# Moving the second image's group statistics into the first image's last tiles, and splitting the last tiles' value products

## The chip, the cores and the metric

The kernel runs on one core of a Trainium2 chip. Its time is the device time of one execution in microseconds (us). The median of three runs is given, and one further execution is recorded by the hardware profiler. A difference of about 0.2% can be told from none.

## The reference, cut to what matters

Two images of 256 channels and 64 x 64 positions, fp32, pass through two residual layers, each on the group-normalised x:

```python
def _gn(v, G=32, eps=1e-5):              # 32 groups of 8 channels
    g = v.reshape(B_, G, C_ // G, H_, W_)
    m = jnp.mean(g, axis=(2, 3, 4), keepdims=True)
    s = jnp.var(g, axis=(2, 3, 4), keepdims=True)
    return ((g - m) / jnp.sqrt(s + eps)).reshape(v.shape)

# layer 0: 8 heads of 32 channels over all 4096 positions
qkv = jnp.einsum('bchw,oc->bohw', x, qkv_w) + qkv_b[None, :, None, None]
...
attn_weights = jax.nn.softmax(attn_logits, axis=-1)
out = jnp.einsum('bhij,bhcj->bhci', attn_weights, v)

# layer 1: two attentions in small blocks, and a convolution
ctx = _sa(blockify(fq), blockify(fk), blockify(v), oh, ow)   # 64 positions of equal place in the 8 x 8 blocks
feats = _bn_relu(_c1x1(ctx, lr_W_w), lr_W_scale, lr_W_shift)
...
qx = _bn_relu(_c1x1(_bn_relu(_c1x1(feats, sr_fq1_w), ...), sr_fq2_w), ...)
kx = _bn_relu(_c1x1(_bn_relu(_c1x1(feats, sr_fk1_w), ...), sr_fk2_w), ...)
vx = _c1x1(feats, sr_fv_w)
ctx2 = _sa(qx, kx, vx, DH, DW)                               # within each 8 x 8 block
feats2 = _bn_relu(_c1x1(ctx2, sr_W_w), sr_W_scale, sr_W_shift)
...
return rate1 * out_att + rate2 * out_conv                    # out_conv: 3 x 3 convolution of q, k, v

x = x + _L0_conv_ref(_gn(x), L0_conv_qkv_w, L0_conv_qkv_b, 8)
x = x + _L1_conv_ref(_gn(x), ...)
```

## The kernel before

The images are done one after the other. An image is held as eight tiles `x_b_t` of 128 partitions x 2 channel halves x 512 positions (eight rows of the picture), from `xpool`, which has nine buffers; so tiles of the second image can be loaded as those of the first come free.

Per image the stages are these. `group_stats` takes bn_stats (L321) of each half tile, 16 in all, aggregates them (L325), sums over the eight channels of a group with a small product on TensorE (`pm`, L328), forms the spread on VectorE (L328, L332 to L334), sums that over the group (`pv`, L337), and takes Sqrt on ScalarE (ACT, L340) and a reciprocal (L341). `normalise` (L366) then writes `xn`, 16 instructions. `project0` makes `p_wk` and `p_wq` (L416), `attention0` is the long attention over 4096 positions (L545, L551, L560, L597). `layer1_first` makes the first block attention, and `layer1_second` the rest: the second block attention in eight tiles t, and the convolution in 16 turns of `conv_step` (a strip s of a quarter of the image, and one of four output phases q), with the normalised image in `xp`. `xn` and `xp` share the single buffer of `apool`.

A tile of `layer1_second` goes so, by its names on TensorE: `phq`, `prq` (two products for the queries, L1354 and L1363, each followed by a ReLU on ACT, L1142), a turn of the convolution, `phk`, `prk` (the keys), `sp` (scores, L1081), `pvs` (values, L1060), a second turn, `at` (two transposes of the softmax, L1111), `pc` (softmax times values, L1129, one product for each half m of the channels, each followed by a ReLU into `res` on ACT), a third turn. The softmax lies between: maximum and subtraction on VectorE (L1099, L1101), exp on ACT (L1102), sum, reciprocal and product on VectorE (L1104 to L1106). `bd` copies (L1120) bring the transposes to SBUF. Values are copied from their bank half by half, on ACT (L1065) or VectorE (L1067). Tile 7 of the first image has one turn only, the last (strip 3, q 3), and tile 7 of the second has none.

A turn is eight matmuls times four (`mm`, L996), for which POOL makes the operand (`col`, L982, and `v`, L986) one turn ahead; afterwards ACT copies a part (L1001), VectorE makes `z` (L1002 to L1005) and adds it to two x tiles (L1017, L1021, L1023). ACT adds the border's corrections (`conv_edges`, L1030). When a strip's four turns are done, `give` (L1330) adds the attention's `res` to x, and SP writes it out.

The order is written out by hand for TensorE alone (`tc.manual_schedule`, inside `layer1_second`); on the other engines a scheduler orders the instructions, with `tc.issue_after` as a bound from below. The work for the second image that belongs to the seam is the generator `following`: its steps are taken in tile 7 of the first image, the first (loads, the 16 statistics and the aggregates) before `at`, the second (`pm`, the spread) between the two `pc` products, through the argument `between` of `group_attention`, and the third (`pv`, Sqrt, reciprocal) behind them. PSUM in `layer1_second` is four banks for `mm` and four for all else; `project0` has eight.

Of the kernel before, what the change touches and what calls it, by code (L numbers as in the profile page):

```python
# [40 lines left out]
def direct_layers(ctx: ExitStack, tc: tile.TileContext, a: dict, out: bass.AP, bad: bass.AP):  # L41
# [17 lines left out]
    def w4(shape, name, dtype=F32):  # L59
        return work.tile(shape, dtype, tag="w4", name=name)  # L60
# [4 lines left out]

    def load_x(b):
        tiles = []
        for t in range(NT):
            xt = xpool.tile([P, KC, T], F32, tag="x", name=f"x_{b}_{t}")
            nc.sync.dma_start(  # L70
                out=xt,
                in_=a["x"][b, :, t * T : (t + 1) * T].rearrange("(k p) n -> p k n", p=P),
            )
            tiles.append(xt)
        return tiles
# [912 lines left out]

    def conv_step(b, xts, wf, v, s, q, pacc):


        mm = pacc.tile([P, 2, 4, STRIP], F32, tag="acc", name=f"mm_{b}_{s}_{q}")
        for r in range(4):
            for m in range(2):
                for k in range(KC):
                    nc.tensor.matmul(  # L996
                        mm[:, m, r, :], wf[:, k, 4 * r + q, m * P : (m + 1) * P], v[r // 2][:, r % 2, k, :],
                        start=k == 0, stop=k == KC - 1,
                    )
        z = w4([P, 2, 2, STRIP], f"z_{b}_{s}_{q}")  # L1000
        nc.scalar.copy(z[:, 1], mm[:, :, 1, :])  # L1001
# [44 lines left out]

    def group_attention(nm, q, k, tokens, wv, out, busy=False, apart=False, more=None, between=None):

# [6 lines left out]

        def values(half):
            pv = bank([P, 2, C], f"pvs_{nm}_{half}")
            for i in range(2):
                for c in range(KC):
                    nc.tensor.matmul(  # L1060
                        pv[:, i, :], tokens(c, 2 * half + i), wv[:, c, :], start=c == 0, stop=c == KC - 1
                    )
            dst = vs[:, 2 * half : 2 * half + 2, :]
            if half == 0 or busy or apart:
                nc.scalar.copy(dst, pv)  # L1065
            else:
                nc.vector.tensor_copy(dst, pv)  # L1067
# [4 lines left out]

        sp = bank([P, 4, 64], f"sp_{nm}")
        def place_of(t, par):
            return sp[64 * par : 64 * par + 64, t, :], slice((4 * par + t) * 64, (4 * par + t) * 64 + 64)
# [18 lines left out]
        if not first:  # L1094
            values(0)
        if not apart:
            values(1)
# [25 lines left out]
        if apart:  # L1123
            values(1)
        yield
        for m in range(KC):
            pc = bank([P, T], f"pc_{nm}_{m}")
            for w in range(4):
                nc.tensor.matmul(  # L1129
                    pc[:, w * P : (w + 1) * P], vs[:, w, m * P : (m + 1) * P],  # L1130
                    bd[:, w].rearrange("p a i -> p (a i)"), start=True, stop=True,
                )
            out(m, pc)
            if m == 0 and between:
                between()

# [147 lines left out]
    def layer1_second(b, xts, feats, mean, rstd, shift, pacc, following):  # L1284
# [30 lines left out]

        def conv():
            nonlocal done, wf
            if wf is None:
                wf = fetch_conv_weights(b)
            if done + 1 < len(turns):  # L1320
                ahead[done + 1] = conv_transform(b, xp, *turns[done + 1])
            conv_step(b, xts, wf, ahead.pop(done), *turns[done], pacc)
            done += 1

        def give(n):
# [3 lines left out]
            for m in range(KC):  # L1329
                kept["given"] = nc.vector.scalar_tensor_tensor(  # L1330
                    res[:, m, :], res[:, m, :], wts["rate1"], xts[n][:, m, :], ALU.mult, ALU.add
                )
                if final:
                    (nc.scalar if m else nc.sync).dma_start(out=halves[:, m, :], in_=res[:, m, :])
# [9 lines left out]
        for t in range(NT):  # L1344
# [4 lines left out]

            def branch(one, two, col1, col2, nm):  # L1350
                hid = w4([P, KC, T], f"h{nm}_{nt}")
                ph = [bank([P, T], f"ph{nm}_{nt}_{m}") for m in range(KC)]
                for k, m in ((0, 0), (0, 1), (1, 0), (1, 1)) if t == 0 else ((0, 0), (1, 0), (0, 1), (1, 1)):
# [3 lines left out]
                    if k == KC - 1:  # L1357
                        bn_relu(hid[:, m, :], ph[m], col1, m)
                res = w4([P, KC, T], f"r{nm}_{nt}")
                pr = [bank([P, T], f"pr{nm}_{nt}_{m}") for m in range(KC)]  # L1360
# [8 lines left out]

            with tc.manual_schedule(engines={mybir.EngineType.PE}):  # L1370
                q = branch("fq1", "fq2", V_FQ1, V_FQ2, "q")
# [6 lines left out]
                if 0 in spots.get(t, ()) and (b or t > 2):  # L1378
                    conv()
                if b == 0 and t == NT - 1:  # L1380
                    for n in sorted(results):
                        give(n)
                k = branch("fk1", "fk2", V_FK1, V_FK2, "k")
                if b == 0 and t == 2:
# [3 lines left out]
                def to_res(m, pc, res=res):  # L1388
# [7 lines left out]
                    nt, q, k, lambda c, w, f=f: f[c][:, w * P : (w + 1) * P], wts["fv"], to_res, apart=t + 1 < NT,  # L1396
                    between=lambda: next(then) if b == 0 and t == NT - 1 else None,
                )
                next(parts)
                if 1 in spots.get(t, ()):  # L1400
                    conv()
                if t < 2 and b == 0:
                    pending = parts
                else:
                    next(parts)
                    if b == 0 and t == NT - 1:
                        next(then)
                    next(parts, None)
                    if b == 0 and t == NT - 1:
                        next(then)  # L1410
                if 2 in spots.get(t, ()):
                    conv()
            if b == 0 and t == 1:
# [13 lines left out]
            for n in sorted(n for n in results if done >= 4 * (n // 2 + 1)):  # L1427
                give(n)


    ahead = {}

    def following():

        ahead.update(xts=load_x(1), w0=load_layer0(1))
        with tc.issue_after(kept["given"].ins):
            steps = group_stats(ahead["xts"], "l0_1")
            next(steps)
        yield
        next(steps)  # L1440
        yield
        ahead["stats"] = next(steps)
        yield

    for b in range(B):
        xts = x_first if b == 0 else ahead["xts"]
        w0 = w0_first if b == 0 else ahead["w0"]
        with tc.tile_pool(name=f"ps0_{b}", bufs=8, space=PSUM) as psum["ps"]:
            mean, rstd = list(group_stats(xts, "l0_0"))[-1] if b == 0 else ahead["stats"]
            xn = apool.tile([P, KC, N], F32, tag="A", name=f"xn_{b}")  # L1450
            for t in range(NT):
                for k in range(KC):
                    normalised = normalise(xn[:, k, t * T : (t + 1) * T], xts[t][:, k, :], k, mean, rstd)
            fold = fold_scores() if b == 0 else iter(())
            next(fold, None)
            held = project0(b, xn, w0)
            next(fold, None)
# [570 lines left out]
```

## Time and profile before

| what | us |
|---|---|
| median of three runs (lowest to highest) | 3057.96 (3056.49 to 3058.67) |
| the profiled execution, its own time | 3062.01 |
| span of its trace, first to last instruction | 3060.1 |
| TensorE busy in the span | 2979.3 |
| VectorE, ScalarE, POOL busy | 2455.9, 2340.2, 832.1 |
| last turn of the first image on TensorE, start | 1520.23 |
| first product of the second image, start | 1552.39 |
| last `pc` of the second image, start | 3049.04 |

The mean granted clock of TensorE is 0.991. In the lines of the profile PE is TensorE, DVE VectorE, ACT ScalarE, SP the engine whose queue carries most transfers, and L with a number is the line in the kernel's text. In a timeline the columns are the start, the time taken, the engine and line, the operation with what it writes and reads, how many instructions are put together in the row, and in brackets how long the engine stood idle before them and what it waited for. TensorE is busy for 97% of the span, so a microsecond counts if TensorE stands still in it, or works slower than at full clock.

### The profile page before, as it was taken

The numbers are of one execution on the slowest core, as the hardware profiler recorded it, in microseconds if no ns is written. First come the engines' busy times: TensorE is split into PE (matmuls) and PEld (weight loads), VectorE is DVE, ScalarE is ACT, GpSimd is POOL, SyncE is SP. The second block draws the span as 40 slices with busy tenths as digits, with TensorE's granted clock in tenths as the row PEclk, the third lists the DMA queues.
The fourth block names the chain that finished last, engine by engine and source line by source line (L and its number), as shares of the span: only waits on it lengthen the run. The fifth ranks groups of instructions, "written<-read, shape, count | busy, mean of one in ns | idle before, by whom it ended". The sixth has DMA issues, their size and how long they took to land. (4 is left out here: it accounts for less than half of the span.)

```text
span 3060.1 us, 63941 instructions
## 1 busy us (share of the span) xinstructions
PE 2979.3 (97%) x25129; PEld 1859.9 (61%) x25129; DVE 2455.9 (80%) x3122; ACT 2340.2 (76%) x3266; POOL 832.1 (27%) x918
## 2 busy tenths in 40 slices
PE   7999999999999999999989999999999999999998
PEld 4565556655556556577755555666555565576765
DVE  4598998989899999856556989989988899835543
ACT  2699999999999984623237999999999999834333
POOL 1022222322223230155301222222222222306440
PEclk9999999999999999999999999999999999999999
DMA  7978789787897661230159787797878976700000
GB/s 259 274 137 180 150 163 175 153 172 157 176 181 159 140 135 42 73 131 28 42 193 274 134 169 163 159 181 146 174 162 167 183 160 131 170 5 4 21 15 22
DMA packets 244149, 425.01 MB, mean 139 GB/s; under 512 B 98889, under 2 KB 109949, under 8 KB 241661
## 3 DMA queue, kind: packets, MB, share of 16 engines
q0 software_dynamic: 94720, 237.57, 40.2%
q1 hardware_dynamic: 148972, 182.99, 21.6%
q8 instruction: 199, 3.26, 0.4%
q14 instruction: 114, 0.93, 0.1%
q10 hardware_dynamic: 144, 0.26, 0.0%
HBM read 119.55 MB, written 68.39 MB: 61 GB/s over the span
## 5 line engine op out<-in xcount | busy, mean ns | idle before, releaser
L551 ACT ACTIVATE es<-ring 128x512 f32<-128x512 f32 (+2 forms) x1572 | 1203.1, 904 | 29.9 <-PE ring L545 21.7
L545 PE MATMUL ring<-q,k 128*128 128x512 f32 x4096 | 1081.8, 407 | 11.2 <-ACT v L551 4.9
L597 DVE TENSOR_TENSOR e<-e,es 128x1024 f32<-128x1024 f32 (+1 forms) x956 | 1036.2, 1148 | 22.5 <-ACT es L551 22.2
L545 PEld LDWEIGHTS ring<-q,k 128*128 128x128 f32 x4096 | 733.4, 188 | 379.7 <-ACT es L551 115.7
L551 ACT ACTIVATE v<-ring 128x512 f32<-128x512 f32 (+2 forms) x1024 | 780.4, 899 | 23.8 <-PE ring L545 13.4
L560 PE MATMUL av<-es,v 128*32 128x256 f32 (+1 forms) x9684 | 725.2, 389 | 0.0
L597 DVE TENSOR_TENSOR e<-e,v 128x1024 f32<-128x1024 f32 (+1 forms) x636 | 670.1, 1112 | 22.4 <-ACT v L551 21.5
L560 PE MATMUL av<-v 128*32 128x256 f32 (+1 forms) x6188 | 498.0, 389 | 0.0
L560 PEld LDWEIGHTS av<-es,v 128*32 128x32 f32 x9684 | 328.3, 109 | 265.3 <-issue 105.5
L560 PEld LDWEIGHTS av<-v 128*32 128x32 f32 x6188 | 221.2, 109 | 171.2 <-issue 72.8
L996 PE MATMUL mm<-v,wf 128*128 128x256 f32 x1024 | 227.6, 380 | 1.5 <-DVE z L1005 1.5
L607 POOL DMA_DIRECT2D es<-es x118 | 100.7, 853 | 461.6 <-ACT es L551 411.4
L996 PEld LDWEIGHTS mm<-v,wf 128*128 128x128 f32 x1024 | 193.3, 190 | 36.8 <-issue 9.8
L986 POOL TENSOR_TENSOR v<-col 128x512 f32<-128x512 f32 x128 | 165.7, 1319 | 178.4 <-ACT rk_sr L1142 38.7
L1001 ACT COPY z<-mm 128x512 f32<-128x512 f32 x32 | 18.7, 586 | 183.3 <-PE mm L996 183.3
L607 POOL DMA_DIRECT2D acc<-es x118 | 119.5, 1018 | 113.8 <-ACT v L551 35.2
L605 POOL DMA_DIRECT2D es<-es x20 | 11.4, 569 | 495.2 <-ACT es L551 404.6
L607 POOL DMA_DIRECT2D es<-v x72 | 61.3, 852 | 290.8 <-ACT v L551 287.2
L1002 DVE TENSOR_TENSOR z<-z,mm 128x512 f32<-128x512 f32 x32 | 22.0, 687 | 140.1 <-ACT z L1001 139.7
L607 POOL DMA_DIRECT2D v<-es x112 | 114.3, 1020 | 17.7 <-ACT es L551 8.4
L607 POOL DMA_DIRECT2D acc<-v x78 | 75.1, 963 | 76.0 <-ACT es L551 31.1
L982 POOL TENSOR_TENSOR col<-xp 128x1152 f32<-128x1152 f32 x32 | 69.6, 2174 | 66.5 <-DVE xp L1420 55.1
(254 smaller groups left out, 2665.5 us busy)
## 6 DMA issues: line engine op xcount, KB each, us to landing
acc<-es POOLq DMA_DIRECT2D x128, 512.0 KB, 6.4
acc<-v POOLq DMA_DIRECT2D x84, 512.0 KB, 6.2
es<-es POOLq DMA_DIRECT2D x138, 256.0 KB, 4.3
v<-es POOLq DMA_DIRECT2D x132, 256.0 KB, 5.1
k<-wk_halves SPq DMA_DIRECT2D x64, 512.0 KB
q<-wq_halves SPq DMA_DIRECT2D x256, 128.0 KB
v<-v POOLq DMA_DIRECT2D x90, 256.0 KB, 5.0
es<-v POOLq DMA_DIRECT2D x84, 256.0 KB, 3.9
```

The source lines that it names most:

```text
L545: touch(nc.tensor.matmul(sc[:, i, :], held["k", g // 2][:, j * P : (j + 1) * P], held["q", g, u // 2][:, u % 2, :], start=True, stop=True, ...
L551: nc.scalar.activation(dst, sc, AF.Exp, scale=SC0), set(range(at % BANKS, at % BANKS + m))
L560: note(nc.tensor.matmul(dst[HD0 * u : HD0 * u + HD0, n], lhs, rhs(u)[:, n], start=start, stop=stop))
L597: nc.vector.tensor_add(dst[:, s, :], dst[:, s, :], src)
L605: nc.gpsimd.dma_start(out=dst, in_=src)
L607: nc.gpsimd.dma_start(out=dst, in_=src, accum_op=ALU.add)
L982: (nc.gpsimd.tensor_add if plus else nc.gpsimd.tensor_sub)(col, cols(one), cols(two))
L986: (nc.gpsimd.tensor_add if plus else nc.gpsimd.tensor_sub)(dst, rows(one), rows(two))
L996: nc.tensor.matmul(mm[:, m, r, :], wf[:, k, 4 * r + q, m * P : (m + 1) * P], v[r // 2][:, r % 2, k, :], start=k == 0, stop=k == KC - 1,)
L1001: nc.scalar.copy(z[:, 1], mm[:, :, 1, :])
L1002: nc.vector.tensor_add(z[:, 0], z[:, 1], mm[:, :, 0, :])
```

## The change

`following` becomes a generator of many small steps, which the tiles 6 and 7 of the first image take at fixed places. In these two tiles the order on VectorE is written out as well as that on TensorE. The tiles 0 to 6 of the second image are loaded ahead as before, and its tile 7 is read straight into the last part of `xn`, where it is normalised in place; a second copy of it goes into an x tile later, for the residual sum. The statistics come in three lots: tiles 0 to 2 in tile 6 after the scores, tiles 3 to 6 ahead of the `z` of turn 14, and tile 7 with the aggregates and the mean ahead of the `z` of turn 15. `pv`, Sqrt and reciprocal follow the key's first product, and the 16 normalises stand at several places in tile 7's attention: five before the maximum, one after the softmax's product, and so on.

In tile 7 of both images the value products are split around the transposes: three of the four places before, the last one behind the copies of `bd`, and ACT copies both halves. In most other tiles, the second `bd` copy stands ahead of the `z` of the turn that follows it.

In the program that comes of it, tile 7's two statistics stand with the first lot on VectorE and both aggregates with the second; the third lot is the mean and the spread. ACT has two table loads in tile 7 of the first image, and none at the start of the second image's attention. The five fetches of layer 0's weights stand earlier on POOL's queue, and the fetches of `k` on SP's stand ahead of six of the writes of `q`'s halves.

```diff
...
@@ -63,9 +63,9 @@
         return psum["ps"].tile(shape, F32, tag="bank", name=name)
 
 
-    def load_x(b):
+    def load_x(b, ts=range(NT)):
         tiles = []
-        for t in range(NT):
+        for t in ts:
             xt = xpool.tile([P, KC, T], F32, tag="x", name=f"x_{b}_{t}")
             nc.sync.dma_start(
                 out=xt,
@@ -986,7 +986,7 @@
             (nc.gpsimd.tensor_add if plus else nc.gpsimd.tensor_sub)(dst, rows(one), rows(two))
         return v
 
-    def conv_step(b, xts, wf, v, s, q, pacc):
+    def conv_step(b, xts, wf, v, s, q, pacc, behind_products=None):
 
 
         mm = pacc.tile([P, 2, 4, STRIP], F32, tag="acc", name=f"mm_{b}_{s}_{q}")
@@ -997,6 +997,8 @@
                         mm[:, m, r, :], wf[:, k, 4 * r + q, m * P : (m + 1) * P], v[r // 2][:, r % 2, k, :],
                         start=k == 0, stop=k == KC - 1,
                     )
+        if behind_products:
+            behind_products()
         z = w4([P, 2, 2, STRIP], f"z_{b}_{s}_{q}")
         nc.scalar.copy(z[:, 1], mm[:, :, 1, :])
         nc.vector.tensor_add(z[:, 0], z[:, 1], mm[:, :, 0, :])
@@ -1044,7 +1046,7 @@
 
     SC1 = C ** -0.5
 
-    def group_attention(nm, q, k, tokens, wv, out, busy=False, apart=False, more=None, between=None):
+    def group_attention(nm, q, k, tokens, wv, out, busy=False, apart=False, more=None, split=False, fill=None):
 
 
 
@@ -1053,15 +1055,21 @@
 
         vs = w4([P, 4, C], f"vs_{nm}")
 
-        def values(half):
-            pv = bank([P, 2, C], f"pvs_{nm}_{half}")
-            for i in range(2):
+        pvs = {}
+
+        def values(half, places=range(2)):
+            if half not in pvs:
+                pvs[half] = bank([P, 2, C], f"pvs_{nm}_{half}")
+            pv = pvs[half]
+            for i in places:
                 for c in range(KC):
                     nc.tensor.matmul(
                         pv[:, i, :], tokens(c, 2 * half + i), wv[:, c, :], start=c == 0, stop=c == KC - 1
                     )
+            if places[-1] == 0:
+                return
             dst = vs[:, 2 * half : 2 * half + 2, :]
-            if half == 0 or busy or apart:
+            if half == 0 or busy or apart or split:
                 nc.scalar.copy(dst, pv)
             else:
                 nc.vector.tensor_copy(dst, pv)
@@ -1071,6 +1079,7 @@
             values(0)
 
         sp = bank([P, 4, 64], f"sp_{nm}")
+
         def place_of(t, par):
             return sp[64 * par : 64 * par + 64, t, :], slice((4 * par + t) * 64, (4 * par + t) * 64 + 64)
 
@@ -1093,7 +1102,9 @@
             yield
         if not first:
             values(0)
-        if not apart:
+        if split:
+            values(1, range(1))
+        elif not apart:
             values(1)
         nm4 = small.tile([P, 4], F32, tag="nm4", name=f"nm4_{nm}")
         nc.vector.tensor_reduce(nm4, sp, AX.X, ALU.max, negate=True)
@@ -1122,6 +1133,8 @@
             )
         if apart:
             values(1)
+        elif split:
+            values(1, range(1, 2))
         yield
         for m in range(KC):
             pc = bank([P, T], f"pc_{nm}_{m}")
@@ -1131,8 +1144,8 @@
                     bd[:, w].rearrange("p a i -> p (a i)"), start=True, stop=True,
                 )
             out(m, pc)
-            if m == 0 and between:
-                between()
+            if fill:
+                fill(m)
 
     def product(pt, wt, src, m, last=True):
         for k in range(KC):
@@ -1313,13 +1326,13 @@
         }
         images = {1: range(5), 3: (5, 6), 4: (7,)} if b == 0 else {0: (3, 4), 1: (5,), 2: (6,), 3: (7,)}
 
-        def conv():
+        def conv(behind_products=None):
             nonlocal done, wf
             if wf is None:
                 wf = fetch_conv_weights(b)
             if done + 1 < len(turns):
                 ahead[done + 1] = conv_transform(b, xp, *turns[done + 1])
-            conv_step(b, xts, wf, ahead.pop(done), *turns[done], pacc)
+            conv_step(b, xts, wf, ahead.pop(done), *turns[done], pacc, behind_products)
             done += 1
 
         def give(n):
...
@@ -1347,7 +1360,7 @@
                 feats[k][:, 8 * t : 8 * t + 8].rearrange("p o d e -> p (o d e)") for k in range(KC)
             ]
 
-            def branch(one, two, col1, col2, nm):
+            def branch(one, two, col1, col2, nm, between=None):
                 hid = w4([P, KC, T], f"h{nm}_{nt}")
                 ph = [bank([P, T], f"ph{nm}_{nt}_{m}") for m in range(KC)]
                 for k, m in ((0, 0), (0, 1), (1, 0), (1, 1)) if t == 0 else ((0, 0), (1, 0), (0, 1), (1, 1)):
@@ -1356,6 +1369,8 @@
                     )
                     if k == KC - 1:
                         bn_relu(hid[:, m, :], ph[m], col1, m)
+                if between:
+                    between()
                 res = w4([P, KC, T], f"r{nm}_{nt}")
                 pr = [bank([P, T], f"pr{nm}_{nt}_{m}") for m in range(KC)]
                 for k in range(KC):
@@ -1367,7 +1382,15 @@
                     bn_relu(res[:, m, :], pr[m], col2, m)
                 return res
 
-            with tc.manual_schedule(engines={mybir.EngineType.PE}):
+            E = mybir.EngineType
+            seam = b == 0 and t == NT - 1
+            near = b == 0 and t >= NT - 2
+
+            def step(n=1):
+                for _ in range(n if near else 0):
+                    next(then)
+
+            with tc.manual_schedule(engines={E.PE, E.DVE} if near else {E.PE}):
                 q = branch("fq1", "fq2", V_FQ1, V_FQ2, "q")
                 if pending:
                     next(pending)
@@ -1376,11 +1399,11 @@
                 for tt in images.get(t, ()):
                     to_image(tt)
                 if 0 in spots.get(t, ()) and (b or t > 2):
-                    conv()
-                if b == 0 and t == NT - 1:
+                    conv(step if seam else None)
+                if seam:
                     for n in sorted(results):
                         give(n)
-                k = branch("fk1", "fk2", V_FK1, V_FK2, "k")
+                k = branch("fk1", "fk2", V_FK1, V_FK2, "k", step if seam else None)
                 if b == 0 and t == 2:
                     conv()
                 res = w4([P, KC, T], f"res_{nt}")
@@ -1394,22 +1417,27 @@
 
                 parts = group_attention(
                     nt, q, k, lambda c, w, f=f: f[c][:, w * P : (w + 1) * P], wts["fv"], to_res, apart=t + 1 < NT,
-                    between=lambda: next(then) if b == 0 and t == NT - 1 else None,
-                )
+                    split=t + 1 == NT, fill=lambda m: step(3 if seam else 0),
+                )
+                if seam:
+                    step(5)
                 next(parts)
+                step()
                 if 1 in spots.get(t, ()):
-                    conv()
+                    conv(None if t < 2 and b == 0 else lambda: next(parts))
+                elif b or t > 1:
+                    next(parts)
                 if t < 2 and b == 0:
                     pending = parts
                 else:
-                    next(parts)
-                    if b == 0 and t == NT - 1:
-                        next(then)
+                    if seam:
+                        step(2)
                     next(parts, None)
-                    if b == 0 and t == NT - 1:
-                        next(then)
+                    if seam:
+                        for _ in then:
+                            pass
                 if 2 in spots.get(t, ()):
-                    conv()
+                    conv(step)
             if b == 0 and t == 1:
 
 
@@ -1426,31 +1454,58 @@
             results[t] = res
             for n in sorted(n for n in results if done >= 4 * (n // 2 + 1)):
                 give(n)
+            if b == 0 and t == NT - 3:
+                next(then)
 
 
     ahead = {}
 
     def following():
 
-        ahead.update(xts=load_x(1), w0=load_layer0(1))
-        with tc.issue_after(kept["given"].ins):
-            steps = group_stats(ahead["xts"], "l0_1")
-            next(steps)
+        last_tile = slice((NT - 1) * T, N)
+        xts = ahead["xts"] = load_x(1, range(NT - 1))
         yield
-        next(steps)
+        st = Stats(xts, "l0_1")
+        for t in range(NT - 5):
+            for k in range(KC):
+                st.tile(k, t)
         yield
-        ahead["stats"] = next(steps)
+        xn = ahead["xn"] = apool.tile([P, KC, N], F32, tag="A", name="xn_1")
+        nc.sync.dma_start(out=xn[:, :, last_tile], in_=a["x"][1, :, last_tile].rearrange("(k p) n -> p k n", p=P))
+        ahead["w0"] = load_layer0(1)
+        views = st.xts = [*xts, xn[:, :, last_tile]]
+        for t in range(NT - 5, NT - 1):
+            for k in range(KC):
+                st.tile(k, t)
         yield
+        both = slice(0, KC)
+        for k in range(KC):
+            st.tile(k, NT - 1)
+        st.aggregate(both)
+        st.means(both, bank([P, KC], "pm_l0_1"), nc.vector.tensor_copy)
+        st.spread(both)
+        yield
+        pv = bank([P, KC], "pv_l0_1")
+        st.variances(both, pv)
+        st.deviations(both, pv)
+        for t in range(NT):
+            for k in range(KC):
+                yield
+                normalise(xn[:, k, t * T : (t + 1) * T], views[t][:, k, :], k, st.mean, st.rstd)
+        yield
 
     for b in range(B):
-        xts = x_first if b == 0 else ahead["xts"]
+        xts = x_first if b == 0 else ahead["xts"] + load_x(1, range(NT - 1, NT))
         w0 = w0_first if b == 0 else ahead["w0"]
         with tc.tile_pool(name=f"ps0_{b}", bufs=8, space=PSUM) as psum["ps"]:
-            mean, rstd = list(group_stats(xts, "l0_0"))[-1] if b == 0 else ahead["stats"]
-            xn = apool.tile([P, KC, N], F32, tag="A", name=f"xn_{b}")
-            for t in range(NT):
-                for k in range(KC):
-                    normalised = normalise(xn[:, k, t * T : (t + 1) * T], xts[t][:, k, :], k, mean, rstd)
+            if b == 0:
+                mean, rstd = list(group_stats(xts, "l0_0"))[-1]
+                xn = apool.tile([P, KC, N], F32, tag="A", name="xn_0")
+                for t in range(NT):
+                    for k in range(KC):
+                        normalised = normalise(xn[:, k, t * T : (t + 1) * T], xts[t][:, k, :], k, mean, rstd)
+            else:
+                xn = ahead["xn"]
             fold = fold_scores() if b == 0 else iter(())
             next(fold, None)
             held = project0(b, xn, w0)
```

More of the change, by code (lines that the diff above doesn't have):

```diff
@@ L1329, in give @@
             for m in range(KC):
-                kept["given"] = nc.vector.scalar_tensor_tensor(
+                nc.vector.scalar_tensor_tensor(
                     res[:, m, :], res[:, m, :], wts["rate1"], xts[n][:, m, :], ALU.mult, ALU.add
```

## The prediction

> **What bounds the kernel now.** I read the page's busy table first, then TensorE's waits, then TensorE's timeline at the seam between the images and at the end, and last the granted clock. TensorE is busy nearly all the time, so only what it stands still for, or runs slowly in, can be won.
>
> ```profile
> PE 2979.3 (97%) x25129; PEld 1859.9 (61%) x25129; DVE 2455.9 (80%) x3122; ACT 2340.2 (76%) x3266; POOL 832.1 (27%) x918
> ```
>
> TensorE's waits between 1525 and 1575 us (engine, line, releaser, total, times, longest) sum to 7.8 us, and each has its place in the timeline:
>
> ```profile
> PE p_wk L416 <- ACT rstd_l L340: 3.1, 1, 3.1
> PE pm_l L328 <- DVE mv_l L325: 2.1, 1, 2.1
> PE at_sr L1111 <- DVE e_sr L1106: 1.1, 1, 1.1
> PE pc_sr L1129 <- DVE bd L1120: 1.0, 1, 1.0
> PE sp_sr L1081 <- ACT rk_sr L1142: 0.5, 1, 0.5
> ```
>
> ```profile
> 1540.90 0.44 PE L1111 MATMUL at_sr<-ident,e_sr 128*128 128x128 f32 x2 [1.12 <-DVE e_sr L1106]
> 1542.38 2.05 PE L1129 MATMUL pc_sr<-bd,vs_sr 128*128 128x128 f32 x8 [1.04 <-DVE bd L1120]
> 1546.58 0.56 PE L328 MATMUL pm_l<-mv_l,group 128*128 128x2 f32 x2 [2.15 <-DVE mv_l L325]
> 1546.99 2.05 PE L1129 MATMUL pc_sr<-bd,vs_sr 128*128 128x128 f32 x8
> 1552.39 15.73 PE L416 MATMUL p_wk<-xn,wqk 128*128 128x512 f32 x32 [3.13 <-ACT rstd_l L340]
> ```
>
> The 16 statistics (L321) stand on VectorE at 1533–1546, in and behind tile 7's softmax; `at` and `pc` wait for that softmax, `pm` for the aggregate, the second image's first product for the deviation. The clock makes it worse (columns: PE, PEld, DVE, ACT, POOL busy, then the granted clock, DMA share, GB/s):
>
> ```profile
> 1542.00:1543.00 1.00, 0.62 (x3) 0.65 (x4) 0.97 (x3) 0.00 (x0) 0.00 (x0) 0.64 0.10 32
> 1543.00:1555.00 12.00, 6.73 (x22) 4.94 (x22) 8.84 (x22) 3.10 (x4) 0.00 (x0) 0.50 0.12 44
> 1556.00:1560.00 4.00, 4.00 (x11) 1.85 (x10) 4.00 (x9) 1.73 (x3) 0.00 (x0) 1.00 0.00 0
> ```
>
> From 1542.4 to 1555.5 TensorE runs at half speed. Hence the first 32 `p_wk` records take 15.73 us where 32 full-speed ones take 13.9 (8 in 3.60).
>
> **The change part by part.**
>
> *Statistics out of the tail.* 16 bn_stats at 0.60 spacing (3.06 for 5) and two aggregates, 0.59, leave 1533–1546 for VectorE's gaps before it:
>
> ```profile
> 1502.64 0.42 DVE L1120 COPY bd<-at_sr 64x256 f32<-64x256 f32 x1 [4.85 <-PE at_sr L1111]
> ...
> 1515.09 0.69 DVE L1002 TENSOR_TENSOR z<-z,mm 128x512 f32<-128x512 f32 x1 [5.49 <-ACT z L1001]
> ...
> 1528.01 0.69 DVE L1002 TENSOR_TENSOR z<-z,mm 128x512 f32<-128x512 f32 x1 [7.62 <-ACT z L1001]
> ```
>
> The source speaks of tiles 0–2, 3–6 and 7. In the changed program's order on VectorE the last tile's two statistics have slipped into the first lot and both aggregates into the second; the third lot is only the mean's copy and three 0.16 us steps. So: lot 1, 8×0.60 from 1497.8, ends 1502.6 against 1502.64: no delay. Lot 2, 8×0.60+0.59 from 1509.8, ends 1515.3: +0.2 on the `z` of turn 14, whose last read of its bank (1518) comes 2.2 before turn 15 starts on TensorE (1520.2): hidden. Lot 3 needs `pm`, which stands after turn 15 (1527.3): the mean and spread end about 1528.4, +0.4 on that `z`, which nobody on TensorE waits for. `pm` and `pv` cost TensorE about 0.3 each (bounds 0.15 and 0.56; nearest: two transposes, 0.38).
>
> *Deviation ahead of the softmax.* `pv` stands after `phk`, at 1530.9. ACT then runs table load, Sqrt, edges, `rk`. Its row of before:
>
> ```profile
> 1549.88 1.28 ACT L340 ACT_TABLE_LOAD   x1
> ```
>
> hk ends 1531.8, table 1533.1, rstd 1533.35, three edges 1534.1, two `rk` (0.75 each) 1535.6. `prk` ends 1534.8, so `sp` waits for `rk` 0.5 in all, as before, and ends 1536.7. Five normalises (0.46 spacing) run on VectorE at 1534.0–1536.45, before `sp` is ready. Maximum and subtraction end 1537.65. ACT meanwhile did five edges (1536.8) and the second table load, back to Exp, 1538.1; exp ends 1538.5, 0.45 later than without that load. Sum, reciprocal, product: 1539.65. That second load replaces the one at the attention's start (1637.70), where it is worth 0.1 at most.
>
> *Values split.* Twelve `pvs` records end 1539.5, transposes at 1539.7 (wait 0.2 for 1.1), four more `pvs` to 1540.95 under the copies of `bd`, 1541.06 (one normalise, 0.46, stands ahead of them), then both `pc` products back to back, 1541.1–1543.3 (wait 0.15 for 1.0; 1.1 each at full clock). The values' last copy, now on ACT (0.59), ends 1541.6 with no one waiting.
>
> *Start of image 1.* Ten normalises follow `bd`; six are done. The first product waits for a bank that ACT frees with tile 7's last result: 1543.35 + 0.78 = 1544.1, so it starts at 1544.2 against 1552.39: 8.2 won. With the idle cut from 7.8 to about 1.8 and at most 1.2 in any 3.4 us, I take the clock as full: `p_wk` keeps 13.9 for 15.73, another 1.8. **Seam: 10.0**.
>
> *Rule against row, the clock.* Here the longest wait before the drop at 1542.4 was 1.12 us; the waits in the 3.4 us before it sum to 2.15. [...] removing them need not restore the clock, and 1.8 at `p_wk`, 1.0 at `pc` and 0.6 at `pvs` would stay lost: 3.4 less. By the row, accumulated idle suffices, and its removal restores it. I take the row.
>
> *Rule against row, the table.* [...] The row says 1.28. [...] I take the row, the same operation in this kernel.
>
> *The end.* Tile 7 of image 1 is split too. There `pc` stood 1.49 for `bd`, behind the values' copy:
>
> ```profile
> 3047.44 0.69 DVE L1067 COPY vs_sr<-pvs_sr 128x512 f32<-128x512 f32 x1 [1.25 <-PE pvs_sr L1060]
> 3048.04 0.85 DVE L1120 COPY bd<-at_sr 64x256 f32<-64x256 f32 x2
> 3049.04 2.02 PE L1129 MATMUL pc_sr<-bd,vs_sr 128*128 128x128 f32 x16 [1.49 <-DVE bd L1120]
> ```
>
> The product ends 3046.19, so transposes go to 3046.4, `bd` 3046.85–3047.7, `pc` at 3047.85: **1.2**.
>
> *At nothing:* `bd` copies moved ahead of `z` in the other tiles (TensorE waited for `bd` only in tiles 7); five weight fetches on POOL's queue, 4.2 us, moved from 1511 to about 1494.6, where POOL is done (1494.5) and next has nothing; an extra 512 KB for tile 7, on SP, beside DMA engines idle from 1488; fetches of `k` ahead of six `wq` writes on SP (by my estimate the half they read lands 1 us before; if not, SP waits, and TensorE has 70 us of projections before it needs them).
>
> Sum 10.0 + 1.2 + 0.1 = 11.3, off the profiled execution's 3062.0. The median of the runs is 3058.0, 4.0 below it at the same work, so the same 11.3 off it: **3046.7**.
>
> **The rivals.** (1) *Won only in part.* The idle left near 1535–1540 still lets one window halve[...]. For: the chain has under 0.5 us of slack at `sp`, exp and `bd`, each on another engine. Against: windows with 1.2 idle; no other place in the trace halves at that.
>
> (2) *The lots aren't hidden.* Rows of `x` beside POOL's transform stretched from 0.42 to 1.49 us (1465.42). If lot 2 did so: 8×1.49 = 11.9 for 4.8, 7 late, 2 of slack: 5 back, 3051.7: within what can be told. Against: POOL ends at 1494.5 and both lots come after it.
>
> (3) *Slower: the last tile comes late.* It is fetched straight into `xn`, over `xp`, whose last reader, POOL's `col` of turn 15, ends at 1486.8. Its statistics stand in lot 1, not where the source has them, ahead of tile 6's `bd` copies; behind these are `pc` of tile 6, `z` and turn 14. From 1501.4 on each microsecond of lateness is one on TensorE, and stands on top of a cold clock. To lose 11.3 and 6.1 more it must land after 1519, 32 us from its issue: 3064 or more. Against: the four transfers ahead of it on SP (two results out, two x in, 2 MB) went at some 380 GB/s and were done at 1487.5, and SP has nothing else until 1517, so I estimate 1491. It decides only if the write waits for another reader than `col`.
>
> (4) *It doesn't do what it says*: the slipped last tile is such a case; at 1491 it costs nothing, and helps turn 15.
>
> **How the numbers follow.** Main case 0.72, 3044.5–3048.5 (run spread 2.2, `sp`–exp chain 1). Rival 1 0.14; more than 14 won 0.03, if the attention's start gains from fresher `xn`; rival 2 0.07; rival 3 0.04. About 0.2%, 6.1 us, is what a measurement here can tell from no change, so faster means below 3051.8: 0.72 + 0.14 + 0.03 = 0.89, less 0.01 for a rival 1 with both losses; same 0.08; slower 0.04. The range, 3043.0 to 3053.0, takes in rivals 1 and 2.
>
> **What would show it.** Right: p_wk starts about 8 us earlier and 32 records take 13.9; granted clock 1.00 through 1530–1560; `pm`'s and rstd's waits gone; two table loads near 1532 and 1537, none at the attention's start; the last `pc` without its 1.49. Wrong: a clock of 0.50 anywhere after 1535; `sp` waiting over 1 us for `rk`, or `at` for exp; `bd_6` after 1503; the end of tile 7 as before.

## The result, and the profile after

| | before | after |
|---|---|---|
| median of 14 runs each (us) | 3061.39 (3054.71 to 3066.24) | 3049.60 (3047.64 to 3055.16) |
| span of the profiled execution | 3060.1 | 3047.8 |
| seam: start of turn 15 to start of `p_wq` on TensorE | 1567.96 - 1520.23 = 47.73 | 1557.34 - 1519.82 = 37.52 |
| tail: start of the last `pvs` to start of the last `pc` | 3049.04 - 3043.61 = 5.43 | 3036.91 - 3032.79 = 4.12 |

The changed kernel is faster: the ratio to before is 0.9967 (95% interval 0.9960 to 0.9974), that is 10.1 us less of 3061.4 (8.0 to 12.2). The seam and the tail are measured from one instruction on TensorE to another, because turn 15 itself starts anywhere from 1516.35 to 1521.14 in the traces told of here (the late tile's aside), whatever comes after it. The seam gave 10.2 us and the tail 1.3. Between the two, from the start of `p_wq` to that of the last `pvs`, the traces differ by 0.2 (1475.65 and 1475.45), so nothing else in the change shows. A second trace of the kernel after has a seam of 37.52 again; that of the kernel before stands on one trace.

TensorE's waits of the kernel after, around the seam, in the columns of those shown of before (7.8 us there, 1.5 from turn 15 on here; the wait for `vs` belongs to tile 6):

```profile
PE p_wk L416 <- ACT res_sr L1155: 0.9, 1, 0.9
PE sp_sr L1090 <- ACT rk_sr L1155: 0.4, 1, 0.4
PE pc_sr L1142 <- ACT vs_sr L1073: 0.2, 1, 0.2
PE pc_sr L1142 <- DVE bd L1131: 0.2, 1, 0.2
```

Its timeline on TensorE: `pm` and `pv` come without a wait, the transposes stand behind twelve value records, and the first 32 `p_wk` records take 14.00 us for 15.73.

```profile
1526.72 0.28 PE L328 MATMUL pm_l<-mv_l,group 128*128 128x2 f32 x2
1530.38 0.28 PE L337 MATMUL pv_l<-d_l,group 128*128 128x2 f32 x2
...
1539.04 0.44 PE L1122 MATMUL at_sr<-ident,e_sr 128*128 128x128 f32 x2
1539.32 1.03 PE L1066 MATMUL pvs_sr<-wt_fv,feats 128*128 128x256 f32 x4
1540.52 2.10 PE L1142 MATMUL pc_sr<-bd,vs_sr 128*128 128x128 f32 x16 [0.17 <-DVE bd L1131]
1543.50 14.00 PE L416 MATMUL p_wk<-xn,wqk 128*128 128x512 f32 x32 [0.87 <-ACT res_sr L1155]
```

Its stretches (third number from the end: the granted clock) stay at full speed, as does the whole of 1520 to 1560, where before fell to 0.50 for 13.6 us:

```profile
1538.00:1542.00 4.00, 3.68 (x23) 2.79 (x22) 3.81 (x10) 1.40 (x3) 0.00 (x0) 1.00 0.06 19
1542.00:1546.00 4.00, 3.13 (x12) 1.68 (x11) 4.00 (x9) 1.76 (x3) 0.00 (x0) 1.00 0.13 46
```

VectorE's timeline of the kernel after has the statistics where its gaps were. Each of these two lots runs into the instruction that it had to leave room for, with hardly any of the gap left over:

```profile
1497.30 3.65 DVE L321 BATCH_NORM_STATS2 stats_l<-x 128x6 f32<-128x512 f32 x6
1500.86 1.27 DVE L321 BATCH_NORM_STATS2 stats_l<-xn 128x6 f32<-128x512 f32 x2
1502.23 0.86 DVE L1131 COPY bd<-at_sr 64x256 f32<-64x256 f32 x2
...
1509.21 4.84 DVE L321 BATCH_NORM_STATS2 stats_l<-x 128x6 f32<-128x512 f32 x8
1513.96 0.59 DVE L325 BATCH_NORM_AGGREGATE mv_l<-stats_l 128x2 f32<-128x48 f32 x2
1514.68 0.69 DVE L1004 TENSOR_TENSOR z<-z,mm 128x512 f32<-128x512 f32 x1
```

And the tail, on TensorE, in the kernel after: 0.18 where `pc` had waited 1.49.

```profile
3035.70 1.03 PE L1066 MATMUL pvs_sr<-wt_fv,feats 128*128 128x256 f32 x4
3036.91 2.10 PE L1142 MATMUL pc_sr<-bd,vs_sr 128*128 128x128 f32 x16 [0.18 <-DVE bd L1131]
```

### The profile page after: what moved, and what is told of

It is laid out like the page before. It is cut to its first block, busy times and chain, and to the rows that moved or that the text cites. A ratio compares the mean times of both kernels' runs of the same rounds, so it can differ in the third digit from the quotient of the medians.

```text
span 3047.8 us, 63942 instructions
## 1 busy us (share of the span) xinstructions
PE 2972.1 (98%) x25129; PEld 1856.3 (61%) x25129; DVE 2452.3 (80%) x3120; ACT 2341.8 (77%) x3268; POOL 832.3 (27%) x918
## 3 DMA queue, kind: packets, MB, share of 16 engines
q0 software_dynamic: 94720, 237.57, 40.4%
```

## The experiments

My theory was that the seam's 10 us are idle time of TensorE plus the half clock that this idle time causes; the rivals gave the clock to something else, or the gain to one part of the change alone. All seams below are in the measure of the table, 37.5 after and 47.7 before.

**Only the split taken back.**

```diff
-        if split:
-            values(1, range(1))
-        elif not apart:
+        if not apart:
             values(1)
...
-        elif split:
-            values(1, range(1, 2))
```

> The kernel after, but with all 16 value records ahead of the transposes in both tiles 7 (ACT still copies both halves). Measures: the seam is from the start of turn 15 on TensorE to the start of p_wq (47.7 us before, 37.5 after); the tail is from the start of the last pvs to the end of the span (16.5 before, 15.0 after). My theory, the split is worth only what the bd copies take on VectorE: transposes 0.75 later at the seam and 1.0 in the tail, pc waiting about 1.0 for bd in each; seam 38.2, tail 16.0, granted clock 1.00 throughout. Rival A, the split is what keeps the clock up: clock 0.50 somewhere between tile 7's transposes and p_wk, seam 39.9 or more. Rival B, the first p_wk waits for the normalises and not for pc: seam 37.5 as before.

Seam 37.93, so the split is worth 0.4 there, less than the 0.7 expected; the clock stays at 1.00 through the seam. In the tail `pc` starts 4.98 after `pvs` (5.43 before, 4.12 after): of the 1.31 won, 0.45 come from ACT copying the second half and 0.86 from the split. To the end of the span, as the expectation measures it, the tail is 15.84 (16.49 before, 15.01 after; 16.0 expected).

```profile
PE pc_sr L1138 <- DVE bd L1129: 1.0, 1, 1.0
PE p_wk L416 <- ACT res_sr L1151: 0.9, 1, 0.9
PE sp_sr L1090 <- ACT rk_sr L1151: 0.4, 1, 0.4
```

Rival A falls: the waits of 1.04 and 0.87 stand 2.0 us apart, which makes at most 1.4 us of idle time in any 3.4, and leave the clock alone. Rival B falls by little, since the seam is only 0.4 longer; but `p_wk` waits the same 0.87 for tile 7's last ReLU, and starts 0.4 later, as `pc` ends 0.4 later.

**Only the split, on the kernel before.** The same split in the kernel before, and nothing else.

```diff
-        if not apart:
+        if split:
+            values(1, range(1))
+        elif not apart:
             values(1)
...
         if apart:
             values(1)
+        elif split:
+            values(1, range(1, 2))
...
-            if half == 0 or busy or apart:
+            if half == 0 or busy or apart or split:
```

> The kernel before with the split of the values alone (statistics, deviation and normalises stay where they were). Theory: at the seam the softmax, held among the statistics, still ends late, so the transposes wait longer (about 1.5 for 1.1) for the same thing; only the values' copy of 0.69 leaves VectorE: seam 47.1, clock still 0.50 for four windows; the tail gets its whole gain, 15.0 to 15.2. Rival, the split alone keeps the clock: seam about 44.

Seam 1563.55 - 1516.35 = 47.20, 0.5 won, as expected; from `pvs` to `pc` the tail has its whole gain (4.12). To the end of the span it is 15.46, more than the 15.0 to 15.2 expected: what stands behind `pc` took 11.34 here, 11.06 before and 10.89 after, and no run tells why. At the seam the idle time only moves: `pc` waits 0.18 for `bd` in place of 1.04, but `pm` 2.98 in place of 2.15, since the statistics still end on VectorE when they end. The clock is at 0.50 for three steps of 3.4 us, where four were expected. So at the seam the split alone is worth 0.5.

**One lot instead of three.** All statistics ahead of turn 15's `z`, held behind the last addition of turn 14.

```diff
-                        nc.vector.tensor_sub(dst, dst, zs)
+                        kept["turn"] = nc.vector.tensor_sub(dst, dst, zs).ins
...
-        for t in range(NT - 5):
-            for k in range(KC):
-                st.tile(k, t)
...
-        for t in range(NT - 5, NT - 1):
-            for k in range(KC):
-                st.tile(k, t)
...
-        for k in range(KC):
-            st.tile(k, NT - 1)
+        with tc.issue_after(kept["turn"]):
+            for t in range(NT):
+                for k in range(KC):
+                    st.tile(k, t)
```

> The kernel after with all 16 statistics and both aggregates in one lot, behind the x additions of turn 14 and ahead of the mean. Theory, the lots are needed since one lot doesn't fit VectorE's gap before turn 15's end: 10.2 us from 1520.1 end at 1530.3, pm waits 3.6 on TensorE, seam 41.0 at full clock, and 42.7 if that one gap halves the clock for one window of 3.4 us. Rival, VectorE's gap of 7.6 us at this place covers it: seam 37.5 to 38.

Seam 1560.72 - 1517.97 = 42.75: the number expected with one window at half clock (0.50 from 1529.3 to 1532.8). TensorE waits where it was said to:

```profile
1528.31 0.38 PE L328 MATMUL pm_l<-mv_l,group 128*128 128x2 f32 x2 [3.27 <-DVE mv_l L325]
```

The lots are needed. One gap of VectorE doesn't hold 10 us of statistics.

**The deviation late, the statistics early.**

```diff
-                k = branch("fk1", "fk2", V_FK1, V_FK2, "k", step if seam else None)
+                k = branch("fk1", "fk2", V_FK1, V_FK2, "k")
...
-                    ..., split=t + 1 == NT, fill=lambda m: step(3 if seam else 0),
+                    ..., split=t + 1 == NT, fill=lambda m: step(1 if seam and m == 0 else 0),
...
-                if seam:
-                    step(5)
                 next(parts)
-                step()
+                if not seam:
+                    step()
```

(The two steps behind the softmax go as well.)

> The kernel after with pv, Sqrt and reciprocal behind the first pc product and all normalises behind that (statistics stay in their lots). Theory: the first p_wk starts 1.2 later, waiting about 2.1 for the deviation and two normalises; then, by the idle that adds up (0.2 + 2.1 in 3.4 us, as in the kernel before), the clock halves for a window: seam 38.7 + 1.7 = 40.4. [...] Rival, the early deviation is worth nothing since p_wk waits for tile 7's last result anyway: 37.5.

Seam 1560.41 - 1520.19 = 40.22, within 0.2 of the 40.4 expected of idle time that adds up. The wait and the stretches:

```profile
1541.55 1.14 PE L1142 MATMUL pc_sr<-bd,vs_sr 128*128 128x128 f32 x8
1544.91 15.67 PE L416 MATMUL p_wk<-xn,wqk 128*128 128x512 f32 x32 [2.23 <-ACT res_sr L1155]
```

```profile
1540.00:1545.00 5.00, 2.60 (x20) 2.28 (x20) 1.86 (x5) 3.58 (x5) 0.00 (x0) 1.00 0.18 52
1546.00:1548.00 2.00, 2.00 (x3) 0.73 (x3) 2.00 (x6) 0.00 (x0) 0.00 (x0) 0.50 0.00 0
```

After this single wait of 2.23 us the clock stands at 0.50 for 3.4 us; `p_wk` pays for it with 1.7 us (15.67 for 14.00). The profile puts the wait down to tile 7's last ReLU, which stands on ACT behind the late table load and Sqrt and ends at 1544.62:

```profile
1542.40 1.28 ACT L340 ACT_TABLE_LOAD   x1
```

The first normalise ends later still, at 1544.81, so `p_wk` could not have started before it: the late deviation holds it up in two ways.

**A gap of chosen size.** Ahead of tile 7's maximum stand eleven, thirteen and, in a later run, eight normalises for five.

```diff
-                    next(then)
+                    next(then, None)
...
                 if seam:
-                    step(5)
+                    step(11)
```

(The first two lines let the later places find no step left.)

> The kernel after with eleven normalises, for five, ahead of tile 7's maximum. This makes one gap of chosen size on TensorE: the softmax starts 2.2 later, the transposes wait about 2.0, p_wk starts 1.9 later. Seam 39.4 at full clock. By the row of before (2.15 us of idle in gaps of at most 1.1 halved the clock) the clock should halve for a window or more, seam 41 or more. [...]

> The same with thirteen normalises: the transposes wait about 2.9, p_wk starts 2.8 later. [...] Accumulated idle: clock 0.50 for at least a window of 3.4 us, seam 42 or more.

Seams 1561.28 - 1520.11 = 41.17 and 1559.48 - 1518.19 = 41.29; the transposes wait 2.71 and 2.83. The clock halves in both, to 0.50 for 3.4 us. But the sizes were wrong: eleven cost as much as thirteen. With eleven, ACT's program order has the values' first copy ahead of the second table load, and exp waits for both. The next run tests that.

> The kernel after with eight normalises ahead of the maximum. With eleven, ACT's program order had the values' first copy ahead of the second table load, so exp waited for that copy (it needs two of the products) and then for the load, and the transposes waited 2.7 where I had reckoned 2.0. The same order stands in this program. Theory: that order, not the normalises, sets the wait: 2.6 to 2.8 here too, clock halved for a window, seam 41.0 to 41.3. Rival: VectorE's normalises set it: maximum 0.9 later, transposes wait 0.7, clock 1.00, seam 38.1.

Seam 1559.38 - 1518.21 = 41.17, the wait again 2.71. ACT's timeline with eight:

```profile
1536.50 0.58 ACT L1073 COPY vs_sr<-pvs_sr 128x512 f32<-128x512 f32 x1 [1.97 <-issue]
1537.11 1.28 ACT L1113 ACT_TABLE_LOAD   x1
1538.40 0.42 ACT L1113 ACTIVATE e_sr<-e_sr 128x256 f32<-128x256 f32 x1
```

The load had nothing to wait for after 1534.5, but stands behind a copy that needs two value products. The subtraction ends at 1536.2 (VectorE), exp starts at 1538.4. In the changed kernel the load stands ahead of the copy:

```profile
1536.15 1.28 ACT L1113 ACT_TABLE_LOAD   x1
1537.45 0.42 ACT L1113 ACTIVATE e_sr<-e_sr 128x256 f32<-128x256 f32 x1
1538.11 0.59 ACT L1073 COPY vs_sr<-pvs_sr 128x512 f32<-128x512 f32 x1 [0.25 <-issue]
```

So the wait is set by ACT's order, which nobody wrote down, and three more normalises on another engine were enough to turn it round. The stretches with eight:

```profile
1539.00:1540.00 1.00, 0.00 (x1) 0.01 (x1) 0.93 (x4) 0.00 (x0) 0.00 (x0) 0.78 0.00 0
1540.00:1542.00 2.00, 2.00 (x6) 1.73 (x7) 1.63 (x4) 0.00 (x0) 0.00 (x0) 0.50 0.00 0
1542.00:1543.00 1.00, 1.00 (x5) 0.86 (x4) 1.00 (x4) 0.57 (x1) 0.00 (x0) 0.51 0.00 0
1543.00:1546.00 3.00, 2.13 (x15) 1.71 (x14) 3.00 (x7) 1.57 (x3) 0.00 (x0) 1.00 0.34 87
```

**The table loads taken away.** The square root is left out, and with it both loads.

```diff
-        st.deviations(both, pv)
+        nc.scalar.activation(st.rstd[:, both], pv, AF.Identity, bias=eps)
+        nc.vector.reciprocal(st.rstd[:, both], st.rstd[:, both])
```

> The kernel after with the square root left out (ACT runs Identity for Sqrt, so the normalised second image is wrong in scale), which takes away both table loads of 1.28 us. Theory, the loads lie beside TensorE's work: sp's wait stays 0.4 to 0.5 (rk ends 0.75 after prk in any case), exp is 0.4 earlier, but the transposes stand behind the values' products: seam 37.3 to 37.5. Rival, the loads are on the path: seam 35 to 36.5.

Seam 1555.44 - 1518.24 = 37.20: both loads together cost 0.3 in the kernel after, 0.1 more than my upper figure. They lie beside TensorE's work as long as ACT runs them ahead of the copy.

**The last tile late.** A small product on TensorE reads `xp` behind tile 6's scores, and the load into `xn`, which must wait for it, is done three times in a row.

```diff
...
+        nc.tensor.matmul(bank([P, 2], "late"), group8, kept["xp"][:, 0, PADW - 2, 1:3], start=True, stop=True)
+        xn = ahead["xn"] = apool.tile([P, KC, N], F32, tag="A", name="xn_1")
+        for _ in range(3):
+            nc.sync.dma_start(out=xn[:, :, last_tile], in_=...)
...
```

> The kernel after with the last tile of the second image made late: its load waits for a small product on TensorE behind tile 6's scores and is done three times in a row, so that it lands about 1507 to 1508.5 where VectorE wants it at 1500.9; the two statistics stand ahead of tile 6's bd copies as in the kernel after. By my third rival of the prediction each us late is one on TensorE: pc of tile 6 5.5 us later, and a cold clock on top, 1.7 to 3.4: 7 to 9 us slower than the kernel after. Against it: the idle VectorE of 5.5 to 7.6 us before the next two turns takes it up, and TensorE loses under 2.

From tile 6's `mm` to turn 15 TensorE takes 1527.04 - 1494.67 = 32.37 us, against 1519.82 - 1494.80 = 25.02 after: 7.35 lost, and the seam behind it is 37.51. The run took 3058.99 us. VectorE, then TensorE, in its timeline:

```profile
1496.92 3.65 DVE L321 BATCH_NORM_STATS2 stats_l<-x 128x6 f32<-128x512 f32 x6
1507.13 1.28 DVE L321 BATCH_NORM_STATS2 stats_l<-xn 128x6 f32<-128x512 f32 x2 [6.56 <-DMA xn<-in_x_dram]
1508.33 0.84 DVE L1131 COPY bd<-at_sr 64x256 f32<-64x256 f32 x2
```

```profile
1509.32 3.75 PE L1142 MATMUL pc_sr<-bd,vs_sr 128*128 128x128 f32 x16 [5.55 <-DVE bd L1131]
1512.86 7.47 PE L996 MATMUL mm<-v,wf 128*128 128x256 f32 x32
```

The third rival's price holds, near enough: VectorE stood 6.6 us, and TensorE lost 5.3 by further waiting (5.55 for the 0.23 that this `pc` waited in the kernel after) and 2.0 by half clock (`pc` 3.75 for about 2.1, `mm` 7.47 for 7.07). About 1.2 of the 6.6 fell beside the value products that stand ahead of `pc`. VectorE's idle time before the later turns takes nothing of it up. In the changed kernel the tile comes in time: VectorE takes its statistics at 1500.86 without a wait.

**What is left: the banks.** The first `p_wk` still waits 0.87 for tile 7's last result. The projections of the second image are made inside the first image's pools instead.

```diff
             layer1_second(b, xts, *between, pacc, following)
+            if b == 0:
+                xts_1 = ahead["xts"] + load_x(1, range(NT - 1, NT))
+                held_1 = project0(1, ahead["xn"], ahead["w0"])
```

(The loop then skips the new pool and `project0` for the second image.)

> The kernel after, with the second image's projections of layer 0 made inside the first image's last PSUM pools (four banks for all but the convolution) instead of in a new pool of eight. In the kernel after the first p_wk waits 0.87 for tile 7's last result, though the normalised tiles are there. Theory: that wait is the hand-over of the banks alone, so p_wk follows pc at once; seam 36.6 to 36.7 (37.5 less 0.87), clock 1.00, and the projections behind it (one tile each 1.7 us, drained within 2.5) don't feel four banks for eight; in time 0.9 less, too little to be told. Rival: four banks are too few, the products wait for their copies, and the span gets longer by over 1 us.

> The kernel after, unchanged, on the same chip as the one with open pools, as its measure: seam 37.5, ratio to before 0.9960 to 0.9974.

Seams 1557.51 - 1521.14 = 36.37 with the open pools, 0.2 to 0.3 less than expected, and 1554.82 - 1517.30 = 37.52 without. `p_wk` has no wait, and four banks cost the projections nothing (32 records in 13.90):

```profile
1541.84 2.10 PE L1142 MATMUL pc_sr<-bd,vs_sr 128*128 128x128 f32 x16 [0.17 <-DVE bd L1131]
1543.78 13.90 PE L416 MATMUL p_wk<-xn,wqk 128*128 128x512 f32 x32
```

In time: 3046.68 us, ratio to before 0.9952 (0.9939 to 0.9966), against 3049.17 and 0.9964 (0.9950 to 0.9977) for the changed kernel on the same chip. The trace shows 1.15 us won at the seam; the times agree with it but can't tell it from nothing. Whether a new pool waits as a whole, or only its first bank happened to be the one last in use, this run doesn't show.

## Why the prediction was right

*The sum.* 10.0 was said of the seam, and 10.21 found; 1.2 of the tail, and 1.31 found; 0.1 of the attention's start, and nothing found: in both kernels its first `es` starts 0.53 after the first `ring`, with or without a table load ahead of it. Of 11.3 in all, the trace has 11.5 and the times 10.1 (8.0 to 12.2). The predicted 3046.7 was set against a median of three runs; over 14 runs the kernel before has 3061.4 instead of 3058.0, which is why the measured 3049.6 lies above it with the difference as forecast. It lies above the main case too (3044.5 to 3048.5), and 0.5 below the 3050.1 at which the predicted 3046.7 would stand with the clock's 3.4 us still lost: by the time alone rival 1 and the main case can't be told apart, and it is the seam and the clock that decide for the main case.

The seam's gain has two halves. The waits are 6.5 us less (0.52, 1.12, 1.04, 2.15 and 3.13 before; 0.45, 0.17 and 0.87 after). The half clock of before ran from 1542.29 to 1555.94, and TensorE was busy in 8.28 us of it, at half speed: 4.1 lost. Less 0.3 for `pm` and `pv`, which now hold up other products, that is 10.3. By parts, kernel after kernel: the split alone 0.5 (47.73 to 47.20), the statistics moved as well 7.0 (to the 40.22 of the late deviation), the deviation and the normalises moved as well 2.7 (to 37.52).

*The statistics.* As reckoned, both lots fit: lot 1 ended 0.1 before `bd`, lot 2 delayed `z` by nothing that TensorE saw. That it took the lots, and not just an earlier place, is shown by the one-lot kernel (5.2 us of the seam given back).

*The deviation.* `pm` and `pv` held up the products behind them by 0.15 each, the lower of my bounds, not 0.3. `sp` waited 0.45 for the 0.5 said. exp started 0.42 after the subtraction had ended, for the 0.45 that the second load was to cost. Putting the deviation back costs 2.7: `p_wk` starts 1.0 later (its wait is 1.4 longer, what stands ahead of it is done 0.3 sooner), and 1.7 are half clock.

*The split.* Its share of the seam was small in the working, and is: 0.4. Added to the kernel before, it is 0.5.

*The clock.* From the row of before I took it that idle time adds up, and the runs bear that out. The third column is TensorE's idle time in the step of 3.41 us that ended when the clock fell (the last section tells of these steps):

| kernel | waits ahead of the drop | idle in the step | clock at 0.50 for |
|---|---|---|---|
| after | 0.17 and 0.87 | at most 0.87 | not at all |
| split taken back | 1.04 and 0.87 | at most 1.04 | not at all |
| before | 1.12 and 1.04 | 2.07 | 13.6 us (more waits follow) |
| deviation late | 2.23 | 2.23 | 3.4 us |
| eight, eleven, thirteen normalises | 2.71, 2.71, 2.83 | 2.27, 2.39, 2.48 | 3.4 us each |
| split only, on before | 0.18 and 2.98 | 2.67 | 10.2 us (more waits follow) |
| one lot | 3.27 | 2.38 | 3.4 us |
| last tile late | 5.55 | 3.07 | 6.8 us |

The longest wait of before ahead of the drop was 1.12 us, and with the deviation late one wait of 2.23 us had the half clock behind it. At the seam the clock stayed up with 1.04 us of idle time in a step, and with 1.34 (split only, the step ahead of the one in the table), and fell with 2.07. The 3.4 us that the prediction put on the clock was too low, the loss being 4.1, and its 0.6 at `pvs` was not there to lose: in the kernel before the 16 `pvs` records ran at full clock (3.72). The loss lay at `p_wk` (1.7), at both `pc` (1.0 each) and at `pm` and `pv` (0.4).

*The table loads.* Here too I took the row of before, 1.28 us for a load. In the kernel after, ACT's timeline has the first load right behind the ReLU that ended at 1531.36, and Sqrt right behind the load, 1.3 from the ReLU's end to Sqrt's start:

```profile
1530.58 0.78 ACT L1155 ACTIVATE hk_sr<-phk_sr,vecs 128x512 f32<-128x512 f32 x1 [0.94 <-PE phk_sr L1367]
1531.38 1.28 ACT L340 ACT_TABLE_LOAD   x1
1532.68 0.26 ACT L340 ACTIVATE rstd_l<-pv_l,eps 128x2 f32<-128x2 f32 x1
```

Both loads together cost TensorE 0.3 (37.52 less the 37.20 without them). What I had not reckoned is their place: with eight normalises the values' copy stands on ACT between Sqrt and the second load, which comes directly ahead of exp, and the transposes wait 2.71 us.

*The rivals.* The first (won in part) and the second (lots not hidden) did not come to pass. The third did not either, but its mechanism and its price were shown by making the tile late. In the changed kernel the tile had ten microseconds in hand: the DMA view falls silent at about 1490.1, for the 1491 estimated, and the statistics wanted it at 1500.86.

## What to carry to other kernels

Add up TensorE's waits before pricing them one by one: here a wait of 2.23 us, or two of 1.12 and 1.04 that fell into one step of 3.41 us, had 3.4 us and more of half clock behind them, 1.7 us and more lost, so that removing them gave back more than their length. Work that is not on the path may be moved into an engine's gaps only in pieces that fit them; give the pieces their places in the program order, and look at what stands behind each piece before asking what it costs. When one engine's order is written out and the next one's is not, the second can turn round at a small change.

## What the hardware showed that I had not expected

The half clock came in whole steps, 3.4, 6.8, 10.2 and 13.6 us in eight kernels. Where only waits under 1 us followed at the seam, it was one step, whether the gap was 2.23 us (deviation late) or 3.27 (one lot). So, by my estimate from these steps, such a gap costs its own length and at most about 1.7 us more (half of 3.4); in the kernel before, where waits of 2.15 and 3.13 followed, the clock was down for 13.6 us.

The steps lie on a grid. In the traces of before and after all changes of the clock behind its first rise (19 and 15) are whole multiples of 3.413 us apart, to within 0.01 us. The grid lies differently to the program from trace to trace: it has an edge at 1542.29 before, at 1541.38 after and at 1540.56 with the split taken back, where turn 15 starts at 1520.23, 1519.82 and 1519.12. In the kernel before, both waits ahead of the drop happened to fall into one step; with the split taken back, the two waits fell into two (first number: the length; second: TensorE busy):

```profile
1538.88:1542.29 3.41, 1.34 (x7) 0.65 (x5) 3.25 (x9) 0.00 (x0) 0.00 (x0) 1.00 0.26 77
1542.29:1545.70 3.41, 2.05 (x8) 1.78 (x8) 3.41 (x6) 0.78 (x1) 0.00 (x0) 0.50 0.00 0
```

```profile
1537.15:1540.56 3.41, 2.37 (x13) 1.88 (x12) 2.68 (x7) 1.19 (x3) 0.00 (x0) 1.00 0.13 25
1540.56:1543.97 3.41, 2.54 (x18) 2.08 (x18) 3.41 (x9) 1.56 (x2) 0.00 (x0) 1.00 0.15 52
```

Over the whole of the traces of before and after, behind that first rise, 15 steps at full clock had 2.05 us of idle time or more in them, and half clock followed each. Of eight with 1.40 to 1.86 it followed three (1.76, 1.85 and 1.86), and of those with less, some 1700, none. In the trace with the split taken back it followed one with 0.53 us, in which products of two and three columns stood:

```profile
110.33:113.74 3.41, 2.88 (x20) 2.65 (x20) 0.48 (x1) 1.42 (x5) 0.00 (x0) 1.00 1.04 386
113.74:117.16 3.42, 3.42 (x9) 2.21 (x9) 0.00 (x0) 3.41 (x5) 0.00 (x0) 0.51 1.04 382
```

So in that step idle time was not all that counted; whether it was the narrow products, no run here settles.
